# Reordering the opening of the product-key stage: batch norm first, its operands in the rows of the up-embedding buffer, that buffer loaded late in pieces, and small steps moved between engines

## The chip, the cores and the metric

The kernel runs on one core of one Trainium2 chip. The metric is the device time of one execution in microseconds (us); the times below are medians over runs of the same program. A trace of one profiled execution goes with it.

## What is computed

Two gated layers run over x (8 sequences of 512 tokens, 256 features): in each one a cross-attention and a feed-forward part, each added to x through a tanh gate. The change touches only the last part, a product-key memory of 4096 experts. Cut to that:

```python
def _L1_ffn_ref(x, w_q, bn_gamma, bn_beta, keys, down_embed, up_embed):
    q = jnp.einsum('bnd,de->bne', x, w_q)                       # 2048 columns
    mean = jnp.mean(q, axis=(0, 1)); var = jnp.var(q, axis=(0, 1))
    q = (q - mean) * jax.lax.rsqrt(var + BN_EPS) * bn_gamma + bn_beta
    q = q.reshape(b, n, 2, H, KD).transpose(2, 0, 1, 3, 4)
    sim = jnp.einsum('pbnhd,hkpd->pbnhk', q, keys)               # 2 x 8 heads x 64 keys
    sx, ix = jax.lax.top_k(sim[0], TOPK)
    sy, iy = jax.lax.top_k(sim[1], TOPK)
    all_scores = (sx[..., :, None] + sy[..., None, :]).reshape(b, n, H, TOPK * TOPK)
    scores, pk = jax.lax.top_k(all_scores, TOPK)
    ...
    h = gelu_new(jnp.einsum('bnd,bnhkd->bnhk', x, wd))
    h = jax.nn.softmax(scores, axis=-1) * h
    return jnp.einsum('bnhk,bnhkd->bnd', h, wu)
x = x + jnp.tanh(g_ffn[1]) * _L1_ffn_ref(_layernorm(x, axis=-1), ...)
```

## The kernel before

**The attention phase** (lines 129 to 1003) does everything up to the last feed-forward part, sequence by sequence. It leaves in DRAM the layer-normed tokens with features in the rows (`xT_d`), the residual (`x_d`), and for the first seven sequences the products of all tokens with all 4096 down-embeddings (`h_d`). In SBUF it leaves `gram`, the sum over all tokens of x times x, with the sums of x as a last column.

**The expert matrix is dense.** Experts are numbered 64 i + j. For a block of 256 tokens `gs[n]` holds the activation of all 4096 experts (rows: 64 experts j in each half of the 128 partitions, the halves for different tokens; columns: the 64 rows i times 128 tokens). The activations are multiplied with a dense weight made from the chosen experts, and contracted with `up_sb`, which holds the whole up-embedding (64 rows j, 64 i, 256 features; 4.19 MB) twice: once in partitions 0 to 63 and once in 64 to 127.

**`fold_phase`** opens the stage. It folds w_q, batch norm and keys into one matrix `mk` (256 x 1024) and one row `crow` (1024 constants), so that the scores of a tile of 128 tokens are one product. Its steps, each a group of instructions on TensorE with something behind it:
- `activations(i4)`, 16 of them: one 256 KB load of down-embeddings (`dwl`, two buffers), 32 matmul instructions (line 123) and four GELUs on ScalarE (line 1057). They make the `gs` of the last sequence, whose tokens arrive last (`xl`).
- four rounds over the columns of w_q (`wq`): the products `y` of gram and wq (line 1074), `z` = y times wq on VectorE (1078), and the column sums `sq` (1084).
- the batch norm chain: nine small steps on VectorE and one on GpSimd (1090 to 1104), which end in `ks` and `kh`.
- `pw` (1114), the folded product, copied to `mk` (1119); `pc` (1124), the constants, copied to `crow` (1128).

Two activations stand in each round, four between the batch norm chain and `pw`, and four at the end. The two loads of `up_sb` (line 1133) are issued on GpSimd's queue ahead of `fold_phase`.

**The tile loop.** There are 32 tiles p of 128 tokens, 16 blocks n of two tiles. For a tile: `similar` (scores on TensorE, lines 1162 and 1163, copied by ScalarE), `top` (MAX8 and FIND_INDEX8 over 64 keys, 16 times, 1175 and 1176), `choose` (sums of candidates `al`, then MAX8 and FIND_INDEX8 8 times, the shift `w` in 1195 and its exp), `places` (index arithmetic, softmax, `mlw`, and a transpose on TensorE, 1206 to 1239), `one_hot` four times (1250, 1252 on VectorE, 1253 on GpSimd), `weights_of` four times (`cf` on TensorE, 1263), `weigh` four times (1272). `finish` contracts a block with `up_sb` (`acc`, 1281) and `store` writes it. `fetch` and `apply` load and activate `h_d` of the block after next. The loop at line 1326 writes all of this out in an order that is two tiles ahead: at tile p it does `top`, `choose` and `places` of tile p + 2 and `similar` of tile p + 3. Ahead of the loop stand `similar`, `top`, `choose` and `places` of tiles 0 and 1, and `similar` of tile 2.

TensorE keeps the order in which the program is written (`ORDERED`, a manual schedule); the orders on the other engines and on the DMA queues come from a planner. Every engine carries out its own queue in order.

Of the kernel before, what the change touches and what calls it, by code (L numbers as in the profile page):

```python
# [10 lines left out]
F32 = mybir.dt.float32  # L11
# [25 lines left out]
def kernel(  # L37
# [978 lines left out]
    crow = p2.tile([1, 1024], F32, name="crow")  # L1016
# [15 lines left out]
    def fold_phase(ctx: ExitStack):  # L1032

        wp = ctx.enter_context(tc.tile_pool(name="wp", bufs=2))
        st = ctx.enter_context(tc.tile_pool(name="st", bufs=1))
        ps_h = ctx.enter_context(tc.tile_pool(name="ps_hl", bufs=2, space=PSUM))
        ps_y = ctx.enter_context(tc.tile_pool(name="ps_yf", bufs=2, space=PSUM))
        ps_s = ctx.enter_context(tc.tile_pool(name="ps_st", bufs=1, space=PSUM))

        xl = st.tile([P, NK, S], F32, name="xl")  # L1040
        nc.sync.dma_start(xl, xT_d[:, :, last * S : (last + 1) * S])
        bn_sb = st.tile([P, 32], F32, name="bn_sb")
        nc.scalar.dma_start(bn_sb, bn)
        kT = st.tile([P, 16, 64], F32, name="kT")
        nc.scalar.dma_start(kT, keysT)

        def activations(i4):

            dw = wp.tile([P, NK, 4, 64], F32, name="dwl")
            nc.sync.dma_start(dw, down[:, :, 4 * i4 : 4 * i4 + 4, :])  # L1050
            for i2 in range(2):
                ps = ps_h.tile([P, 2, 2 * P], F32, name="ps_hl")
                for ii in range(2):
                    expert_products(ps[:, ii, :], dw[:, :, 2 * i2 + ii, :], xl)
                for n in range(2):
                    i0 = 4 * i4 + 2 * i2
                    nc.scalar.activation(
                        gs[n][:, i0 : i0 + 2, :], ps[:, :, n * P : (n + 1) * P],
                        AF.Gelu_apprx_tanh,
                    )  # L1060


        sq = ps_s.tile([P, 16, 2], F32, name="sq")
        for n4 in range(4):
            wq = wp.tile([P, NK, 512], F32, name="wq")
            nc.scalar.dma_start(
                wq, pwq[:, 512 * n4 : 512 * (n4 + 1)].rearrange("(k p) n -> p k n", p=P)
            )
            z = wp.tile([P, NK, 512], F32, name="z")
            activations(2 * n4)  # L1070
            for k in range(NK):
                y = ps_y.tile([P, 512], F32, name="y", tag="y")
                for k2 in range(NK):
                    nc.tensor.matmul(
                        y, gram[:, k2, k * P : (k + 1) * P], wq[:, k2, :],
                        start=(k2 == 0), stop=(k2 == NK - 1),
                    )
                nc.vector.tensor_tensor(z[:, k, :], y, wq[:, k, :], ALU.mult)
            activations(2 * n4 + 1)
            for i in range(4):  # L1080
                n = 4 * n4 + i
                for j, (src, by) in enumerate(((z, None), (wq, gram))):
                    for k in range(NK):
                        nc.tensor.matmul(
                            sq[:, n, j : j + 1], src[:, k, i * P : (i + 1) * P],
                            ones[:, 0:1] if by is None else by[:, k, D : D + 1],
                            start=(k == 0), stop=(k == NK - 1),
                        )
        mv = st.tile([P, 16, 2], F32, name="mv")
        nc.vector.tensor_scalar(mv, sq, 1.0 / (NT * P), None, ALU.mult)  # L1090

        sc = st.tile([P, 16], F32, name="bn_sc")
        sh = st.tile([P, 16], F32, name="bn_sh")
        nc.vector.tensor_tensor(sc, mv[:, :, 1], mv[:, :, 1], ALU.mult)
        nc.vector.tensor_tensor(sc, mv[:, :, 0], sc, ALU.subtract)
        nc.vector.tensor_scalar(sc, sc, 0.0, EPS_LN, ALU.max, ALU.add)
        nc.gpsimd.tensor_tensor(sc, sc, mhalf.to_broadcast([P, 16]), ALU.pow)
        nc.vector.tensor_tensor(sc, sc, bn_sb[:, 0:16], ALU.mult)
        nc.vector.tensor_tensor(sh, sc, mv[:, :, 1], ALU.mult)
        nc.vector.tensor_tensor(sh, bn_sb[:, 16:32], sh, ALU.subtract)  # L1100
        ks = st.tile([P, 16, 64], F32, name="ks")
        nc.vector.tensor_tensor(ks, kT, sc.unsqueeze(2).to_broadcast([P, 16, 64]), ALU.mult)
        kh = st.tile([P, 16, 64], F32, name="kh")
        nc.vector.tensor_tensor(kh, kT, sh.unsqueeze(2).to_broadcast([P, 16, 64]), ALU.mult)
        for i4 in range(8, 12):
            activations(i4)
        for h in range(2):
            pw = [ps_y.tile([P, 8, 64], F32, name="pw", tag="y") for _ in range(NK)]
            for q4 in range(2):
                wT = wp.tile([P, 4, D], F32, name="wT")  # L1110
# [18 lines left out]
        for i4 in range(12, 16):  # L1129
            activations(i4)  # L1130
# [269 lines left out]
```

## Time and profile before

| What | Value |
|---|---|
| Median of 3 runs | 4431.82 us (4430.32 to 4437.95) |
| The profiled execution | 4438.74 us |
| Its span, first to last instruction | 4436.9 us |
| Busy: TensorE, VectorE, ScalarE, GpSimd | 85%, 56%, 36%, 14% of the span |
| Attention phase, to the last product of `gram` | 0 to about 3311 us |
| `fold_phase` on TensorE (first `ps_hl` to last) | 3314.6 to 3455.9 us |
| Tiles 0 and 1 ahead of the loop | 3458.6 to 3510.6 us |
| Tile loop, first `cf` to last `acc` | 3510.6 to 4430.6 us |

The page gives each engine's busy share over the span and in 40 slices of 111 us; the stage of this change is the last ten slices. Engines wait for one another by semaphores, so the question in each stretch is which wait ends last. The chain of waits follows that back from the last instruction; the timeline of one engine shows the waits in square brackets with what released them. The profiled execution lies 1.8 us above its span, and 6.9 us above the median.

### The profile page before, as it was taken

To read this page: it belongs to the slowest core of one execution; us is meant where nothing else is said; L and a number is where in the kernel's file an instruction comes from. 1 tells how busy PE (TensorE), PEld (TensorE's weight loads), DVE (VectorE), ACT (ScalarE), POOL (GpSimd) and SP (SyncE) were. 2 spreads that over 40 slices of the span, in tenths; PEclk is the share of its full clock that TensorE was granted. 3 is DMA by queue.
4 is the path that set the end of the run, shared out by engine and by line. 5 is a ranking of instruction groups with operands and counts; after the bars stand their busy time and mean duration, and the time that the engine had idled before them with its cause. 6 is when DMAs were issued, how large, how long until landed. Compare 5 with 4: busy or idle time off the path is not lost.

```text
span 4436.9 us, 74250 instructions
## 1 busy us (share of the span) xinstructions
PE 3779.7 (85%) x30697; PEld 1922.5 (43%) x30697; DVE 2473.8 (56%) x5662; ACT 1580.1 (36%) x2029; POOL 616.8 (14%) x613
## 2 busy tenths in 40 slices
PE   5678788889888998998898898789987589999998
PEld 2223332434334344434334434234445266666667
DVE  3455544454554454455445534553200699999995
ACT  2124343334443443453354343443431123333221
POOL 3210101020011012002001200000000122222222
PEclk7678998899999999999999999998997799999999
DMA  3201122123113313311321321103353022222221
GB/s 97 50 20 39 32 65 53 39 69 103 54 54 105 89 46 99 101 48 54 107 77 51 103 87 46 26 23 81 100 158 95 15 78 84 90 92 92 84 90 42
DMA packets 192254, 314.79 MB, mean 71 GB/s; under 512 B 20190, under 2 KB 145662, under 8 KB 184510
## 3 DMA queue, kind: packets, MB, share of 16 engines
q1 hardware_dynamic: 173468, 239.98, 18.0%
q0 software_dynamic: 15776, 65.02, 5.3%
q10 hardware_dynamic: 2672, 5.04, 0.4%
q8 instruction: 242, 3.96, 0.4%
q14 instruction: 96, 0.79, 0.1%
HBM read 220.93 MB, written 88.24 MB: 70 GB/s over the span
## 4 chain that ended last, share of the span: by engine, by line
PE 37%; DVE 17%; DMA 3%; ACT 1%; issue 1%; POOL 1%; SPq 0%; DVEq 0%; POOLq 0%; ACTq 0%
PE sc L331 10%; PE acc L1281 7%; PE ps_hd L123 6%; DVE nm L348 4%; PE av L391 3%; DVE m L1250 2%; DVE gs L1272 2%; DVE m L1252 2%; PE ps_y L707 1%; PE ps_hl L123 1%; DVE i L1176 1%; PE ps_h L690 1%; PE ps_sim L1162 1%; PE ps_q L293 1%; PE cf L1263 1%
## 5 line engine op out<-in xcount | busy, mean ns | idle before, releaser
L348 DVE TENSOR_REDUCE nm<-sc 128x2 f32<-128x1024 f32 x768 | 939.1, 1224 | 1047.0 <-PE sc L331 1043.2
L331 PE MATMUL sc<-ka,qa 32*128 32x512 f32 x3072 | 960.7, 684 | 297.4 <-DVE nm L348 284.4
L376 ACT ACTIVATE pr<-sc 128x1024 f32<-128x1024 f32 x768 | 785.9, 1024 | 1156.9 <-PE sc L331 1155.1
L331 PE MATMUL sc<-qa,ka 32*128 32x512 f32 x3072 | 917.8, 671 | 21.0 <-ACT pr L376 15.9
L331 PEld LDWEIGHTS sc<-ka,qa 32*128 32x128 f32 x3072 | 261.2, 194 | 722.7 <-DVE nm L348 535.8
L1281 PE MATMUL acc<-up_sb,gs 64*128 64x256 f32 x4096 | 489.9, 394 | 37.6 <-DVE gs L1272 37.6
L123 PE MATMUL ps_hd<-xT,dw 128*64 128x256 f32 x3584 | 439.0, 390 | 17.0 <-DMA dw<-in_down 6.5
L1281 PEld LDWEIGHTS acc<-up_sb,gs 64*128 64x128 f32 x4096 | 405.0, 195 | 93.3 <-DVE gs L1272 39.8
L391 PE MATMUL av<-pr,v 128*32 128x512 f32 x3072 | 436.6, 642 | 7.1 <-ACT pr L376 7.1
L1253 POOL TENSOR_TENSOR m<-m,chT 128x1024 f32<-128x1024 f32 x128 | 256.8, 2006 | 724.1 <-DVE m L1252 513.7
L123 PEld LDWEIGHTS ps_hd<-xT,dw 128*64 128x64 f32 x3584 | 247.1, 139 | 248.8 <-issue 117.9
L331 PEld LDWEIGHTS sc<-qa,ka 32*128 32x128 f32 x3072 | 246.8, 190 | 69.9 <-ACT pr L376 34.6
L823 ACT COPY hb<-ps_hd 128x512 f32<-128x512 f32 x224 | 130.8, 586 | 314.9 <-PE ps_hd L123 289.4
L542 ACT ACTIVATE pd<-mb,aT 128x512 f32<-128x512 f32 (+3 forms) x256 | 129.6, 553 | 211.2 <-PE cav L549 108.7
L391 PEld LDWEIGHTS av<-pr,v 128*32 128x32 f32 x3072 | 62.0, 110 | 320.2 <-issue 298.7
L534 POOL TENSOR_SCALAR_AFFINE_SELECT mb<-mb 128x256 f32<-128x256 f32 x128 | 52.2, 408 | 1010.9 <-DMA mb<-nM_d 572.8
L1263 PE MATMUL cf<-m,m 64*64 64x64 f32 x8192 | 156.1, 228 | 34.5 <-DVE gs L1272 29.0
L1263 PEld LDWEIGHTS cf<-m,m 64*64 64x64 f32 x8192 | 138.9, 141 | 101.4 <-issue 84.8
L1250 DVE TENSOR_TENSOR m<-chT,iota 128x1024 f32<-128x1024 f32 x128 | 169.8, 1326 | 2.0 <-ACT chT L1239 2.0
L569 DVE SCALAR_TENSOR_TENSOR pd<-csc,pd 128x512 f32<-128x512 f32 (+3 forms) x256 | 115.9, 486 | 94.3 <-PE csc L564 77.5
L1196 ACT ACT_TABLE_LOAD x28 | 35.9, 1283 | 366.5 <-DVE w L1195 354.3
L564 PE MATMUL csc<-qT,cT 32*128 32x256 f32 (+3 forms) x512 | 150.8, 567 | 10.8 <-DVE pd L569 7.2
(218 smaller groups left out, 4330.9 us busy)
## 6 DMA issues: line engine op xcount, KB each, us to landing
h_d<-hb SPq DMA_DIRECT2D x224, 256.0 KB
gs<-h_d SPq DMA_DIRECT2D x56, 1024.0 KB
dw<-in_down SPq DMA_DIRECT2D x112, 256.0 KB
w1e<-in_w POOLq DMA_DIRECT2D x16, 1024.0 KB, 5.4
w2e<-in_w POOLq DMA_DIRECT2D x16, 1024.0 KB, 6.3
mb<-nM_d SPq DMA_DIRECT2D x32, 512.0 KB
qk_d<-pk SPq DMA_DIRECT2D x64, 256.0 KB
ws<-in_w SPq DMA_DIRECT2D x56, 256.0 KB
```

The costliest lines, as they stand in the source:

```text
L123: nc.tensor.matmul(ps[64 * q : 64 * q + 64, :], dw[:, k, :], runs[:, :, q, :], start=(k == 0), stop=(k == NK - 1),)
L331: nc.tensor.matmul(sc[:, i, :], lhs[r : r + 32, g, c * P : (c + 1) * P], rhs[r : r + 32, g, :], start=True, stop=True,)
L348: nc.vector.tensor_reduce(self.nm[:, c, 2 * half : 2 * half + 2, g], sc, AX.X, ALU.max, negate=True)
L376: nc.scalar.activation(self.pr[jj], sc, AF.Exp)
L391: nc.tensor.matmul(self.av[32 * j : 32 * j + 32, :], self.va[:, c, h * (self.hd + 1) : h * (self.hd + 1) + 32], pr[j // 2][:, j % 2, :], s ...
L542: nc.scalar.activation(pds[c][:, i, s0:], mb[:, i, s0:], AF.Exp, bias=aT[:, c, h : h + 1])
L564: nc.tensor.matmul(sc[i][:, s0:], cT[r : r + 32, g, s0 : s0 + P], qT[r : r + 32, g, s0:], start=True, stop=True,)
L823: nc.scalar.copy(hb.rearrange("p n i t -> p i n t"), ps.rearrange("p i (n t) -> p i n t", n=2),)
L1250: nc.vector.tensor_tensor(m1, spread(0), grid, ALU.is_equal)
L1253: nc.gpsimd.tensor_tensor(m2, m2, spread(2), ALU.mult)
L1263: nc.tensor.matmul(cf[64 * q : 64 * q + 64, h, s, :], m2[rows, q, s, :], m1[rows, q, s, :], start=True, stop=True,)
L1281: nc.tensor.matmul(accs[n][q], gs[n % 2][rows, i, :], up_sb[rows, i, :], start=(i == 0), stop=(i == 63),)
```

## The change

`fold_phase` moves behind the functions of the tile loop, since it now calls them, and its order is new. Its operands (`xl`, `wq` four times, `z` twice, four `wT`, `kT`, `ks`, `kh`) no longer have buffers of their own but lie in `up_sb`, 4 KB per partition each, which `room(i, ...)` hands out as four of the 64 rows i. So `up_sb` can be loaded only once they are used up: in 16 loads of 512 KB (8 rows i, one half of the partitions), eight after activations 6 to 10 and eight after activations 11 to 15. In this phase the order on SP's queue is as written too.

The rounds have one activation each in place of two. The four activations between the batch norm chain and what follows it are gone; `pc` comes directly after the chain. `crow` becomes three rows of bf16, whose sum is the row (each the rounded rest of the one before), and the third matmul of `similar` takes three rows of bf16 in place of one of f32. Then come two activations, `pw`, and `similar`, `top` and `choose` of tiles 0 and 1; then five activations and `places` of tile 0 with the first eight loads, and the same for tile 1; then `similar` of tile 2.

In the functions of the tile loop four steps change engines: the shift `w` and the softmax product in `mlw` go from VectorE to GpSimd, the casts `kf` and `iv` from VectorE to ScalarE. `choose` makes its sums of candidates on VectorE in both kernels.

```diff
-    crow = p2.tile([1, 1024], F32, name="crow")
+    crow = p2.tile([3, 1024], BF16, name="crow")
+    ones3 = p2.tile([3, P], BF16, name="ones3")
...
-        nc.tensor.matmul(ps, ones[0:1, :], crow[:, cols], start=False, stop=True)
+        nc.tensor.matmul(ps, ones3, crow[:, cols], start=False, stop=True)
...
-        nc.vector.tensor_tensor(w, sc, sc[:, :, 0:1].to_broadcast([P, 8, 8]), ALU.subtract)
+        nc.gpsimd.tensor_tensor(w, sc, sc[:, :, 0:1].to_broadcast([P, 8, 8]), ALU.subtract)
...
-        nc.vector.tensor_copy(kf, ku)
+        nc.scalar.copy(kf, ku)
...
-        nc.vector.tensor_copy(iv, i8)
+        nc.scalar.copy(iv, i8)
...
-        nc.vector.tensor_tensor(
+        nc.gpsimd.tensor_tensor(
             mlw[:, 2, 0, :].rearrange("p (h k) -> p h k", k=8), w,
...
-    for q in range(2):
-        nc.gpsimd.dma_start(up_sb[64 * q : 64 * q + 64], up)
...
+        def room(i, shape):
+            axes = dict(zip("ab", shape))
+            return up_sb[:, 4 * i : 4 * i + 4, :].rearrange(
+                "p x y -> p (x y)"
+            ).rearrange("p (a b) -> p a b", **axes)
+        xl = room(15, (NK, S))
+        nc.sync.dma_start(xl, xT_d[:, :, last * S : (last + 1) * S])
+        wqs = [room(n4, (NK, 512)) for n4 in range(4)]
+        for n4, wq in enumerate(wqs):
+            nc.scalar.dma_start(
...
+            )
+        kT = room(14, (16, 64))
+        wTs = [room(6 + i, (4, D)) for i in range(4)]
+        for i, wT in enumerate(wTs):
+            nc.scalar.dma_start(wT, pwqT[:, 4 * i : 4 * i + 4, :])
...
+        for n4 in range(4):
+            wq = wqs[n4]
+            z = room(4 + n4 % 2, (NK, 512))
+            activations(n4)
...
+        ks = room(10, (16, 64))
+        kh = room(11, (16, 64))
+        for h in range(2):
+            pc = ps_y.tile([P, 512], F32, name="pc", tag="y")
+            nc.tensor.matmul(
+                pc[0:3], ones[:, 0:3], kh[:, 8 * h : 8 * h + 8, :].rearrange("p n i -> p (n i)"),
+                start=True, stop=True,
+            )
+            t0, t1 = (st.tile([3, 512], BF16, name=f"t{i}") for i in range(2))
+            rest = st.tile([3, 512], F32, name="rest")
+            nc.vector.tensor_copy(t0, pc[0:3])
+            nc.vector.tensor_tensor(rest, pc[0:3], t0, ALU.subtract)
+            nc.vector.tensor_copy(t1, rest)
+            nc.vector.tensor_tensor(rest, rest, t1, ALU.subtract)
+            nc.vector.tensor_scalar(rest, rest, ident[0:3, 2:3], None, ALU.mult)
+            for i, t in enumerate((t0, t1)):
+                nc.vector.scalar_tensor_tensor(
+                    rest if i == 0 else crow[:, 512 * h : 512 * h + 512],
+                    t, ident[0:3, i : i + 1], rest, ALU.mult, ALU.add,
+                )
+        activations(4)
+        activations(5)
...
+        for p in range(2):
+            for h in range(2):
+                similar(p, h)
+            for n0 in (0, 8):
+                top(p, n0)
+            choose(p)
+        for p in range(2):
+            for i4 in range(5 * p + 6, 5 * p + 11):
+                activations(i4)
+            places(p)
+            for i in range(32 * p, 32 * p + 32, 8):
+                for q in range(2):
+                    nc.sync.dma_start(
+                        up_sb[64 * q : 64 * q + 64, i : i + 8, :], up[:, i : i + 8, :]
+                    )
+        for h in range(2):
+            similar(2, h)
...
+        phase.enter_context(tc.manual_schedule(engines={mybir.EngineType.SP}))
+        fold_phase(phase)
...
-    for p in range(2):
-        for h in range(2):
-            similar(p, h)
-        for n0 in (0, 8):
-            top(p, n0)
-        choose(p)
-        places(p)
-    for h in range(2):
-        similar(2, h)
     one_hot(0, 0)
```

## The prediction

> **What bounds the kernel now.** I read the page first: its ten last slices are this stage, and in slice 31 TensorE falls to 4 tenths, VectorE to 0, while the DMA engines reach their highest rate. The chain of waits then gives the cause, in pieces of start, length and what ended.
>
> ```profile
> 3314.59 5.38 PE ps_hl L123 x32
> 3319.98 39.10 DMA dwl<-in_down
> 3359.22 5.70 PE ps_hl L123 x32
> ```
>
> An activation of 32 matmul instructions takes 5.4 us at a cold clock; the next but one waits 39 us for 256 KB of `dwl`. The view of the tile `up_sb` says what the DMA engines did meanwhile (two loads issued at 3312, 25.7 and 45.5 us to landing), the table of stretches how fast.
>
> ```profile
> L1133 POOL DMA_DIRECT2D up_sb<-in_up x2: 548/586/624, 3312.1 to 3312.7; - x2
> ...
> DMA to landing us min/median/max: 25.7/35.6/45.5
> ```
>
> ```profile
> 3340.00:3350.00 10.00, 0.00 (x0) 0.00 (x0) 0.00 (x0) 0.00 (x0) 0.00 (x0) 0.50 1.01 212
> ```
>
> No engine works from 3340 to 3350; 16 DMA engines are all busy and move only 212 GB/s. One half of `up_sb`, 4.19 MB, takes 45.5 + 0.6 - 25.7 = **20.4 us**.
>
> The second loss is in the timeline of TensorE: from 3458 to 3510 it is busy 27.5 of 52 us and waits for the VectorE chain of tiles 0 and 1 (`top`, `choose`, `places`), which runs beside nothing.
>
> ```profile
> 3477.76 0.90 PE L1236 MATMUL tr<-ident,mlw 128*128 128x128 f32 x3 [11.53 <-ACT mlw L1233]
> ...
> 3502.17 0.90 PE L1236 MATMUL tr<-ident,mlw 128*128 128x128 f32 x3 [12.38 <-ACT mlw L1233]
> ```
>
> Then the loop. In a stretch of two tiles VectorE is full and TensorE nearly:
>
> ```profile
> 3737.00:3794.00 57.00, 51.84 (x798) 38.31 (x798) 56.72 (x197) 17.43 (x24) 15.21 (x8) 0.94 0.26 88
> ```
>
> The columns are TensorE, its weight loads, VectorE (56.72 of 57), ScalarE, GpSimd. So the loop, 852 us from 3510 to 4362 for 30 tiles' worth of `choose` and `places`, is bound by **VectorE** first, 28.4 us a tile.
>
> **What the Trainium skill says of it.** "SBUF — State Buffer", section "Door 1: The DMA port swizzle": a transfer into 64 partitions reaches 8 of 16 ports, some 218 GB/s; the trace agrees (212). The same page, "Can I just issue two DMAs to hit both halves?": one transfer to each half gains only 6% over one alone, they serialize. The trace has the halves one after the other (4.19 MB in 20.4 us), not interleaved. The same page, "Who interferes with whom": casts in a 2-port mode on VectorE and a running GpSimd instruction block each other. That agrees: `iv` takes 0.19 us at its median and 1.93 where it starts inside a GpSimd product (3746.89, with line 1253 at work from 3746.51). "DMA: Bandwidth & Descriptors", section "Queues, rings and completion order": on each DMA engine a queue's descriptors are taken in ring order. Here it means that a load behind others on SP's queue comes last. The page also has the engines change between queues packet by packet; the 39 us of one `dwl` show that this shares nothing fairly against rows of 64 KB.
>
> **The change, part by part.** First the stretch from the first activation to the first `cf`: 3314.6 to 3510.6, **196 us** before.
>
> *Taken away:* the 39 us (27 idle, plus what stood ready behind). *Hidden:* 52 us of tiles 0 and 1; their VectorE work, some 21 us up to both `choose` (`top` 5.3, `choose` 3.4, twice, and the first scores), now runs beside five activations of 3.6 us. *Uncovered or added:* I lay TensorE's new order out with the durations of before.
>
> - Start: +4. The loads of `wq`, `wT` and `kT` are 4.7 MB, of which before 2 MB (two `wq`, two `wT`) came early, at 3267, and cost TensorE a wait of 5.67 us for `dw`. More may come there now, or later against `xl`: 0 to 8.
> - Four rounds of one activation (3.6), `y` (3.7), `sq` (3.7) and now an open wait for `z` (0.69 us and two handoffs: 1.0), which the second activation used to cover: 12.0, and the first cold +1.7; +1.3 for each of the others for a clock of 0.66 to 0.98 as in 3375 to 3400. Together 13.7 + 3 x 13.3 = 53.6.
> - Batch norm chain, 3409.8 to 3416.6, formerly under four activations: 6.8 bare.
> - `pc` 3.5 (half clock, as before). The splitting into three rows is 7 VectorE steps twice, nearest row the copy of `crow` at 0.68 us: at most 9.5 us, beside activations 4 and 5 (5.4 + 3.6 = 9.0) and `pw` (8.5), since only `similar` needs it. Nothing.
> - Four `similar`: two f32 products 1.91 (measured), the bf16 one 0.25: 8.7.
> - Activations 6 to 10: 18.0.
> - **First new wait.** SP issues the eight pieces after `dwl` 10, that is when activation 8 has freed a buffer. They are 4.19 MB into halves: 20.4 us, and `dwl` 11 is behind them on the same queue. It lands some 23 us after activation 8; activations 9 and 10 cover 7.2. Wait: 16. VectorE's chain for `places` 0 ends about when activation 10 does, so it adds nothing. What waits behind `dwl` 11: all of TensorE's order, the GELUs, `places` 1.
> - A transpose 0.5, activations 11 to 15: 5.7 cold + 14.4 = 20.6 in all.
> - **Second new wait.** Six pieces go out after activation 13, two after 15 (`xl` lies in their rows), and `xTt` of tile 2 is behind them: some 15.5 us after activation 15.
> - `similar` of tile 2, half cold: 6.
>
> Sum: 4 + 53.6 + 6.8 + 3.5 + 9 + 8.5 + 8.7 + 18 + 16 + 20.6 + 15.5 + 6 = 170, against 196: **-26**. Bounds: if the pieces flow at 350 GB/s (near the 363 seen at 3275 to 3280 into all partitions), both waits shrink by some 9: -45. If the buffer is held as a whole, so that pieces wait for every reader of it, each wait grows by some 8: -10. The three `one_hot` of VectorE that ran ahead before can run ahead here too, so the loop begins in the same state.
>
> *The loop, VectorE.* From the groups of lines between 3678 and 4360, 24 of each:
>
> ```profile
> L1212 DVE CAST iv<-i 128x128 bf16<-128x128 uint16 x24 | 23.7, 988 | 0.0
> L1210 DVE CAST kf<-ku 128x128 bf16<-128x128 uint32 x24 | 5.5, 227 | 0.8
> L1229 DVE TENSOR_TENSOR mlw<-w,sm 128x64 f32<-128x64 f32 x24 | 5.4, 225 | 0.8
> L1195 DVE TENSOR_TENSOR w<-psc 128x64 f32<-128x64 f32 x24 | 4.9, 205 | 0.0
> ```
>
> Removed a tile: 0.99 + 0.23 + 0.23 + 0.21 = 1.65 us. Behind `iv` comes MAX8 on one input, so most of its 0.8 us of blocking should go for good. Given back: `hot` waits for `kf`. On ScalarE that is about 0.3 us (the copy in line 1233 of 192 columns has 0.34) and two handoffs of 0.1, against 0.23 before: +0.3. The two products on GpSimd, about 0.3 us each, block the two-input products on VectorE when they meet: +0.3. The `exp` comes some 0.6 later, but its reader `sm` had 1.9 us in hand (3753.2 to 3755.1): nothing. `mlw` is 0.2 later to the transpose, for which TensorE has no wait in the loop. Net 1.05 x 30 = **-30**. Bounds: 1.65 x 30 plus half of VectorE's idle 12 us = -55; all eaten by waits, 0, or worse (below).
>
> *The loop, TensorE.* The bf16 product takes one pass: the skill's "TensorE: Matmul & The Clock Gate", section "Wait — 56ns, not 53.3ns?", has 216 ns for 512 bf16 columns, against 1.05 us in the chain: 0.8 x 2 a tile. The trace shows no bf16 product, so 0.24 to 0.96. TensorE falls from 50.4 to 47.3 us of 57; VectorE is the bound, so it is worth little by itself, but keeps TensorE from taking over.
>
> The last `finish` and `store` don't change. Sum against the profiled execution: 4438.7 - 26 - 30 = 4382.7. It stood 6.9 above the median, so I forecast 4431.8 - 56 = **4376**.
>
> **Rivals.**
> - *The waits are shorter than I think:* -45 and up to -52, 4335. For it: pieces alternate between halves. Against it: the page's 6%. 12%.
> - *The handoffs eat the loop's gain:* VectorE stands in its own order when ScalarE or GpSimd is late. -26 and 0: 4406. For it: an order planned with other durations. 17%.
> - *Slower:* `kf` falls in ScalarE's queue behind the burst of table load, `exp`, table load and two GELUs (1.28 + 0.26 + 1.28 + 2.0 = 4.8 us, from 3780.77). `hot` then waits some 4.5 a tile instead of 1.65 saved: +2.9 x 30 - 26 = +60, 4492. It decides from a wait of 1.65 + 26/30 = 2.5 us a tile. Against it: `ku` ends before the `exp` can begin, so the cast is ready first. 7%.
> - *The load is moved, not hidden:* whole-buffer waits and a colder clock leave the opening as it was, and the loop's gain is eaten: 4432. 4%.
>
> My forecast has 60%. Faster by over 0.2% (9 us, about what a measurement here can tell from no change): 0.6 + 0.12 + 0.17 = 0.89; same 0.04, slower 0.07. The range: 4335 to 4418, from the fast end of both bounds to the opening at -14 with an empty loop; the slower case is left out.
>
> **What would show it.** Right: no wait of 27 us for `dwl` 3; two waits of 13 to 17 us, for `dwl` 11 and for `xTt` of tile 2; a first `cf` near 3485; line 1163 at about 0.25 us, once; VectorE still at 98% in the loop, 27.4 us a tile. Wrong: VectorE idle before `hot` by more than 1 us a tile, a loop over 852 us, or a first `cf` before 3468 or after 3500.

## The result and the profile after

| | before | after |
|---|---|---|
| Median of 4 runs each | 4434.89 us (4430.32 to 4440.0) | 4380.07 us (4373.9 to 4385.84) |
| Ratio, with its 95% interval | 1 | 0.9876 (0.9855 to 0.9897) |
| The profiled execution, and its span | 4438.74, 4436.9 | 4385.84, 4384.1 |
| To the last `ot` product of attention | 3266.8 | 3262.1 |
| From there to the last product of `gram` (`ps_g`) | 44.3 | 38.3 |
| To the first activation of `fold_phase` | 3.5 | 9.7 |
| **The opening**: to the first `cf` | 196.0 | 174.7 |
| **The loop**: to the end of the span | 926.3 | 899.3 |

The changed kernel is 55 us faster by the medians. The profiled executions differ by 52.8 us: 21.3 in the opening, 27.0 in the loop, and 4.7 in attention, which the change doesn't touch (over all the profiled runs below the first activation starts between 3302.5 and 3322.3 us, so 4.7 is no gain). The two rows before the opening cancel out: -6.0 and +6.2.

In the kernel before, TensorE stood 27.0 us for one `dwl`, as its table of waits from 3310 to 3515 says (total us, times, longest):

```profile
PE ps_hl L123 <- DMA dwl<-in_down: 27.6, 2, 27.0
```

The chain of waits of the changed kernel no longer has a 39 us load. It has two of about half that, each behind pieces of `up_sb`:

```profile
3418.76 5.58 DMA up_sb<-in_up
3424.40 17.40 DMA dwl<-in_down
...
3462.90 14.95 DMA xTt<-xT_d
```

TensorE's timeline shows how long it stood for each of them (in brackets, with the releaser), and the small waits in between:

```profile
3321.01 0.38 PE L1198 MATMUL sq<-ones,up_sb 128*128 128x1 f32 x2 [0.67 <-DVE up_sb L1193]
...
3374.43 3.27 PE L1222 MATMUL pc<-up_sb,ones 128*3 128x512 f32 x4 [6.90 <-DVE up_sb L1218]
...
3414.61 10.54 PE L123 MATMUL ps_hl<-up_sb,dwl 128*64 128x256 f32 x80 [2.92 <-ACT gs L1175]
3441.93 12.42 PE L123 MATMUL ps_hl<-up_sb,dwl 128*64 128x256 f32 x96 [16.30 <-DMA dwl<-in_down]
3477.89 3.78 PE L1056 MATMUL ps_sim<-mk,xTt 128*128 128x512 f32 x4 [15.70 <-DMA xTt<-xT_d]
```

From above: the open wait for `z` in a round, the batch norm chain, a wait for the GELUs, and the two waits of 16 us for loads behind the pieces of `up_sb`. The table of stretches (TensorE, its weight loads, VectorE, ScalarE, GpSimd, clock, DMA share, GB/s) shows what holds these two, and then two tiles of the loop:

```profile
3426.00:3442.00 16.00, 0.07 (x2) 0.10 (x4) 10.31 (x6) 0.36 (x2) 7.46 (x3) 0.58 0.96 209
3462.00:3478.00 16.00, 0.30 (x3) 0.11 (x1) 0.00 (x0) 0.92 (x4) 0.00 (x0) 0.63 0.94 199
3738.00:3795.00 57.00, 50.65 (x804) 38.02 (x802) 54.31 (x199) 18.62 (x28) 18.46 (x13) 0.91 0.26 89
```

In both waits the DMA engines are full at about 200 GB/s. In the loop VectorE has fallen from 56.72 to 54.31 us of 57: it is no longer full. The table of waits, from 3660 to 4260 (total us, times, longest), says for what it and TensorE now stand:

```profile
PE tr L1130 <- ACT mlw L1127: 51.7, 11, 4.7
...
DVE s L1069 <- ACT sim L1058: 21.0, 13, 1.9
...
DVE hot L1110 <- ACT kf L1104: 5.5, 22, 0.5
```

The last line was forecast. The first was not: every second tile TensorE waits up to 4.7 us for `mlw` before its transposes, and the scores (`sim`) behind them come late to `top` on VectorE. Over the whole loop, first before and then after:

```profile
PE tr L1236 <- ACT mlw L1233: 19.7, 2, 9.9
...
DVE s L1175 <- ACT sim L1164: 12.5, 9, 2.6
...
PE tr L1130 <- ACT mlw L1127: 89.8, 16, 12.5
...
DVE s L1069 <- ACT sim L1058: 28.7, 18, 1.9
```

The timeline of GpSimd has the cause:

```profile
3753.31 1.90 POOL L1294 TENSOR_TENSOR m<-m,chT 128x1024 f32<-128x1024 f32 x1 [7.50 <-DVE sm L1122]
3755.17 1.27 POOL L1123 TENSOR_TENSOR mlw<-w,sm 128x64 f32<-128x64 f32 x1
```

The softmax product, now on GpSimd, is queued behind a product of `one_hot`, and takes 1.27 us where it takes 0.29 when VectorE leaves it alone.

### The profile page after: what moved, and what is told of

Same layout as the page of the kernel before. It is cut to its first block, busy times and chain, and to the rows that moved or that the text cites. A ratio compares the mean times of both kernels' runs of the same rounds, so it can differ in the third digit from the quotient of the medians.

```text
span 4384.1 us, 74170 instructions
## 1 busy us (share of the span) xinstructions
PE 3707.2 (85%) x30633; PEld 1891.7 (43%) x30633; DVE 2431.7 (55%) x5547; ACT 1599.8 (36%) x2097; POOL 647.7 (15%) x675
## 4 chain that ended last, share of the span: by engine, by line
PE 35%; DVE 17%; DMA 2%; ACT 2%; POOL 2%; issue 1%; SPq 0%; DVEq 0%; POOLq 0%; ACTq 0%
PE sc L331 10%; PE ps_hd L123 6%; DVE nm L348 4%; PE acc L1322 4%; PE av L391 3%; DVE m L1293 2%; DVE gs L1313 2%; PE ps_sim L1056 2%; DVE m L1291 2%; DVE i L1070 1%; PE ps_y L707 1%; PE ps_h L690 1%; PE ps_q L293 1%; PE ps_hl L123 1%; PE ps_p L282 1%
## 5 line engine op out<-in xcount | busy, mean ns | idle before, releaser
L331 PE MATMUL sc<-qa,ka 32*128 32x512 f32 x3072 | 913.7, 668 | 22.1 <-ACT pr L376 16.7
L1322 PE MATMUL acc<-up_sb,gs 64*128 64x256 f32 x4096 | 467.3, 381 | 1.5 <-DVE gs L1313 1.5
L1322 PEld LDWEIGHTS acc<-up_sb,gs 64*128 64x128 f32 x4096 | 389.3, 187 | 49.2 <-DVE gs L1313 1.7
L1056 PE MATMUL ps_sim<-mk,xTt 128*128 128x512 f32 x256 | 151.7, 723 | 15.7 <-DMA xTt<-xT_d 15.7
L1293 DVE TENSOR_TENSOR m<-chT,iota 128x1024 f32<-128x1024 f32 x128 | 161.5, 1262 | 0.0
L1291 DVE TENSOR_TENSOR m<-chT,iota 128x1024 f32<-128x1024 f32 x128 | 157.0, 1227 | 6.9 <-ACT chT L1133 6.9
```

Of the source, the lines that this page charges most:

```text
L331: nc.tensor.matmul(sc[:, i, :], lhs[r : r + 32, g, c * P : (c + 1) * P], rhs[r : r + 32, g, :], start=True, stop=True,)
L1056: nc.tensor.matmul(ps, xt[:, k, :], mk[:, k, cols], start=(k == 0), stop=False)
L1291: nc.vector.tensor_tensor(m1, spread(0), grid, ALU.is_equal)
L1293: nc.vector.tensor_tensor(m2, spread(1), grid, ALU.is_equal)
L1322: nc.tensor.matmul(accs[n][q], gs[n % 2][rows, i, :], up_sb[rows, i, :], start=(i == 0), stop=(i == 63),)
```

## The experiments

All against the kernel before on the same chip. A difference of two ratios counts only where it is clear of their intervals, some 0.001 to 0.003 to each side. The last column is the loop of the profiled run (first `cf` to the end of the span), split into what VectorE was busy and idle. That split is the tool for everything below: the loop is as long as VectorE's busy time plus its idle time, so a change must show in one of them.

| Kernel | Median us | Ratio (95%) | Opening | Loop = busy + idle |
|---|---|---|---|---|
| before | 4429.42 to 4442.93, by chip | 1 | 196.0 | 926.3 = 864.7 + 61.6 |
| the change | 4380.07 | 0.9876 (0.9855 to 0.9897) | 174.7 | 899.3 = 815.6 + 83.7 |
| opening_alone | 4416.15 | 0.9947 (0.9928 to 0.9965) | 177.5 | 933.1 = 872.0 + 61.1 |
| casts_back | 4421.88 | 0.9966 (0.9948 to 0.9983) | 172.3 | 937.4 = 846.8 + 90.6 |
| pool_back | 4442.67 | 1.0014 (0.9999 to 1.0028) | 171.9 | 958.3 = 857.8 + 100.5 |
| row_f32 | 4435.32 | 0.9999 (0.9990 to 1.0008) | 177.6 | 943.3 = 827.3 + 116.0 |
| soft_back | 4386.27 | 0.9890 (0.9858 to 0.9923) | 174.5 | 899.3 = 831.2 + 68.1 |
| late_turn | 4385.41 | 0.9897 (0.9866 to 0.9929) | 171.5 | 909.0 = 838.5 + 70.5 |
| wide_pieces | 4364.89 | 0.9840 (0.9807 to 0.9872) | 155.0 | 898.6 = 816.3 + 82.3 |
| spread_pieces | 4345.78 | 0.9803 (0.9770 to 0.9836) | 138.7 | 900.4 = 816.3 + 84.1 |
| late_turn1 | 4452.08 | 1.0025 (1.0014 to 1.0037) | 174.0 | 964.4 = 852.1 + 112.3 |
| row_turn1 | 4459.44 | 1.0034 (1.0021 to 1.0047) | 179.6 | 965.0 = 851.8 + 113.2 |
| pool_turn1 | 4484.87 | 1.0095 (1.0072 to 1.0118) | 171.5 | 990.1 = 859.4 + 130.7 |
| all_together | 4419.87 | 0.9936 (0.9913 to 0.9959) | 138.2 | 965.8 = 853.2 + 112.7 |

### The opening

**One part alone.** `opening_alone` has the new opening; the four steps go back to their engines and the row to f32.

```diff
-        nc.gpsimd.tensor_tensor(w, sc, sc[:, :, 0:1].to_broadcast([P, 8, 8]), ALU.subtract)
+        nc.vector.tensor_tensor(w, sc, sc[:, :, 0:1].to_broadcast([P, 8, 8]), ALU.subtract)
...
-        nc.scalar.copy(kf, ku)
+        nc.vector.tensor_copy(kf, ku)
...
-        nc.scalar.copy(iv, i8)
+        nc.vector.tensor_copy(iv, i8)
...
-        nc.gpsimd.tensor_tensor(
+        nc.vector.tensor_tensor(
             mlw[:, 2, 0, :].rearrange("p (h k) -> p h k", k=8), w,
...
-        nc.tensor.matmul(ps, ones3, crow[:, cols], start=False, stop=True)
+        nc.tensor.matmul(ps, ones[0:1, :], crow[:, cols], start=False, stop=True)
```

> The changed kernel with the loop's steps as before: the four small steps back on VectorE, the row of constants one row of f32. Only the new opening is left. Theory (two separate gains): the opening and what stands ahead of it is worth 26 us and the loop 27, so about 4434 - 26 = 4408, with a VectorE period of 28.4 us a tile again. Rival (the loop only became faster because it starts with more work done ahead): near 4380.

Measured: ratio 0.9947, so 0.0053 x 4435 = 23.5 us from the opening alone (15 to 32 by its interval); the other 0.0071 x 4435 = 31 us belong to the edits in the loop, given this opening. So both halves of the forecast are real, and the rival, that the loop gained only from its better start, is out. The size of the first half is less sure: in the profiled runs the opening is 18.5 us shorter, its six products of scores having the f32 row again, and the loop 6.8 us longer, since the cast `iv` meets GpSimd more often (33.6 us against 26.6).

**The two new waits.** `wide_pieces` loads into all 128 partitions, for which the input holds the up-embedding twice:

```diff
-                for q in range(2):
-                    nc.sync.dma_start(
-                        up_sb[64 * q : 64 * q + 64, i : i + 8, :], up[:, i : i + 8, :]
-                    )
+                nc.sync.dma_start(up_sb[:, i : i + 8, :], up[:, i : i + 8, :])
```

> The changed kernel with the 16 loads of up_sb into 64 partitions replaced by 8 loads of 1 MB into all 128 (the input is laid out twice, one copy for each half), at the same places of SP's queue. Theory (the two new waits of the opening are as long as the pieces are slow, 205 GB/s into 64 partitions): at about 350 GB/s the 4.2 MB take 12 instead of 20 us, the wait for dwl 11 falls from 16.3 to 8 and that for xTt of tile 2 from 15.7 to 7.5, the time by 16, to about 4364. Rival (the rate comes from the alternation of rows, or the pieces wait for buffers rather than for the DMA engines): both waits stay within 2 us of what they are, and the time at 4380.

Its timeline of TensorE has the same two waits at less than half:

```profile
3433.36 12.08 PE L123 MATMUL ps_hl<-up_sb,dwl 128*64 128x256 f32 x96 [6.52 <-DMA dwl<-in_down]
...
3460.28 3.69 PE L1056 MATMUL ps_sim<-mk,xTt 128*128 128x512 f32 x4 [6.86 <-DMA xTt<-xT_d]
```

Between 3422 and 3434 its DMA engines moved 382 GB/s. So the length of the waits is the bytes of the pieces over their rate: 16.3 + 15.7 became 6.5 + 6.9, and the opening is 19.7 us shorter, where 16 were expected.

`spread_pieces` keeps the 64 partitions and moves the loads apart:

```diff
+            if n4 == 1:
+                piece(48, 56)
+            if n4 == 3:
+                piece(0, 8)
...
+        piece(8, 16)
+        piece(16, 24)
+        after = {7: (24, 32), 8: (32, 40), 9: (40, 48), 10: (56, 60)}
...
+                if i4 in after:
+                    piece(*after[i4])
...
+        piece(60, 64)
```

> The changed kernel with the same 16 loads of 64 partitions, but each pair issued as soon as its rows of up_sb are used up: one in the second round, one in the fourth, two after the second choose, then one after each of activations 7 to 9, the rest after activation 10 and after xTt of tile 2. Theory (the two waits come from eight pieces standing ahead of dwl 11 and of xTt on one queue): both waits of about 16 us go, of which some 3 to 6 us come back as shorter waits for single pieces, and the time falls by 24 to 32, to about 4350. Rival (what the pieces take of the DMA engines is taken from the activations' own loads wherever they stand): as many waits, only shorter each, and the time within 8 us of 4380.

The first wait is gone: activation 11 starts right behind the transposes, and the next wait, of 0.69 us, comes before activation 14. The second is gone too:

```profile
3426.47 10.58 PE L123 MATMUL ps_hl<-up_sb,dwl 128*64 128x256 f32 x96
3437.75 7.13 PE L123 MATMUL ps_hl<-up_sb,dwl 128*64 128x256 f32 x64 [0.69 <-DMA dwl<-in_down]
...
3445.19 1.88 PE L1056 MATMUL ps_sim<-mk,xTt 128*128 128x512 f32 x4
```

The opening is 36.0 us shorter than the change's, more than was expected, and the loop is as it was. 32.0 of them are the two waits; most of the rest comes from the products behind them, which are no longer slow (12.42 to 10.58 us, 3.78 to 1.88). The bytes are the same, and so are the 64 partitions that each piece goes into; what differs is when the pieces are issued. So the 32 us came from eight pieces at a time standing ahead of one small load, and how long such a wait is, their rate decides. The packets of the changed kernel show the order itself: `dwl` 11 was issued at 3424.40, yet none of its packets of 1 KB starts before 3438, when the pieces are nearly through. That another queue for the pieces would have helped was not run. In the kernel before they were on GpSimd's queue, and a `dwl` on SP's took 39.10 us beside them. This is the fastest version that was run: 4345.78 us.

### The loop: one edit undone at a time

`casts_back` puts `kf` and `iv` back on VectorE:

```diff
-        nc.scalar.copy(kf, ku)
+        nc.vector.tensor_copy(kf, ku)
...
-        nc.scalar.copy(iv, i8)
+        nc.vector.tensor_copy(iv, i8)
```

> The changed kernel with the two casts kf and iv back on VectorE. Theory: the loop is bound by VectorE, and iv costs it 0.99 us a tile (0.19 of work and 0.8 blocked by GpSimd), kf 0.23, less 0.25 that it now waits for kf: +0.97 x 30 = +29 us, 4409. Rival (blocking only moves elsewhere): iv counts its 0.19 alone, +5 us, 4385.

The loop is 38.1 us longer: 31.2 of busy time and 6.9 of idle time. That is near the theory and far from the rival, but not by the theory's sum. The cast is blocked at some meetings with GpSimd, though less than before. The group of lines from 3660 to 4260:

```profile
L1106 DVE CAST iv<-i 128x128 bf16<-128x128 uint16 x21 | 12.7, 604 | 0.0
```

Over the loop the two casts take 26.4 us, where the theory had 36.6. The rest came from elsewhere: the `m` steps (the two comparisons of `one_hot`, 1291 and 1293) took 316.7 us against 307.8, and VectorE waited 41.7 us for scores against 28.7.

`row_f32` puts the row back to one f32 matmul, at line 1055 of that kernel:

```diff
-        nc.tensor.matmul(ps, ones3, crow[:, cols], start=False, stop=True)
+        nc.tensor.matmul(ps, ones[0:1, :], crow[:, cols], start=False, stop=True)
```

> The changed kernel with the row of constants as one row of f32 again. TensorE gets some 0.7 us more in each of 64 products, 1.4 us a tile. Theory (VectorE bounds the loop): +0 to +10 us, 4380 to 4390. Rival (TensorE bounds at least half of the loop): +1.4 x 30 = +42, 4422.

The rival was right: the loop's whole gain is lost, and more. The edit only adds 0.73 us to a product on TensorE (1.05 in place of 0.32 from its start to the next), 58 times in the loop: 42 us, and the loop is 44.0 longer. In the table of waits of 3660 to 4260 one sees the path:

```profile
PE tr L1128 <- ACT mlw L1125: 47.0, 10, 4.7
DVE s L1067 <- ACT sim L1056: 42.7, 18, 3.1
```

VectorE waits 42.7 us for the scores, twice what it did. Over the loop its idle time is 32.3 us longer, all of it for scores (61.1 against 28.7), and its busy time 11.7 (the `m` steps). So in the changed kernel **TensorE's order, its work and its wait for `mlw`, sets the pace** together with VectorE. One thing is not separated here: the planner gave VectorE another order too, in which 16 of the 250 `m` steps take over 1.5 us, where the change has 3. So the 44 us are the row together with the order that came with it.

`pool_back` puts the shift `w` and the softmax product of `mlw` back on VectorE:

```diff
-        nc.gpsimd.tensor_tensor(w, sc, sc[:, :, 0:1].to_broadcast([P, 8, 8]), ALU.subtract)
+        nc.vector.tensor_tensor(w, sc, sc[:, :, 0:1].to_broadcast([P, 8, 8]), ALU.subtract)
...
-        nc.gpsimd.tensor_tensor(
+        nc.vector.tensor_tensor(
             mlw[:, 2, 0, :].rearrange("p (h k) -> p h k", k=8), w,
```

> The changed kernel with the shift w and the softmax product of mlw back on VectorE, the casts on ScalarE. Theory: VectorE gets 0.43 us a tile more (+13 us), but TensorE's wait of 4.7 us in every second tile for the transpose behind GpSimd's product goes, and with it most of VectorE's new idle time of 0.78 us a tile (-14 to -23): 4370 to 4380, the same or faster than the changed kernel. Rival (VectorE's work alone counts): +13, 4393.

Both expectations missed: the loop is 59.0 us longer, 42.2 of it busy time, where the rival had 13. The trace shows three things that neither had. The first is on ScalarE and VectorE (one timeline):

```profile
3727.58 1.28 ACT L1090 ACT_TABLE_LOAD   x1 [5.41 <-DVE w L1089]
...
3729.16 0.22 DVE L1121 TENSOR_REDUCE sm<-w 128x8 f32<-128x64 f32 x1 [1.45 <-ACT w L1090]
```

When `w` comes from VectorE, the table load for the exp waits for it, 1.28 us ahead of the exp. `sm`, the sum over that exp, waits 1.45 us a tile, 39.4 in the loop. When `w` comes from GpSimd the load goes out early. But `w` comes from VectorE in the kernel before and in `opening_alone` too, and there `sm` has no wait at all: from the fourth tile of the loop on nine steps stand on VectorE's queue between `w` and `sm`, where in `pool_back`, as in the changed kernel's order, only the two `ku` steps do. So this wait, too, belongs to the edit in this order and not to the edit alone. The second: the product `hot<-hot,iv` takes 774 ns at its mean from 3660 to 4260 and 417 in the changed kernel, 19.5 us in the loop. The third: the softmax product takes 773 ns at its mean in the loop, where it took 224 before, 16.5 us.

`soft_back` is half of that, the softmax product alone:

```diff
-        nc.gpsimd.tensor_tensor(
+        nc.vector.tensor_tensor(
             mlw[:, 2, 0, :].rearrange("p (h k) -> p h k", k=8), w,
```

> The changed kernel with only the softmax product of mlw back on VectorE; the shift w stays on GpSimd. Theory (what made the kernel with both back lose 59 us is the table load of exp, which waits for w on VectorE and holds sm back by 1.45 us a tile): here the table load still goes early, so the time is 4380 to 4395 and VectorE doesn't wait for w before sm. Rival (what cost is the product on VectorE itself, 0.81 us at its mean where GpSimd blocks it, and the hot products beside it): most of the 59 us is here too, 4415 to 4440.

The theory was right: +0.0014 in the ratio, less than the intervals, and a loop of the same 899.3 us. Busy time rises by 15.6 us and idle time falls by as much, since TensorE's wait for `mlw` goes down from 89.8 to 43.4 us in the loop. So, with the other edits in place, the move of this product to GpSimd gave nothing that can be told from none: what VectorE saved came back as its wait for scores (28.7 us against 15.5). VectorE's order is the changed kernel's here with this one step put in, so no other order is mixed in. The loss of `pool_back` came with the move of `w` and the order planned for it.

### Is TensorE's wait worth taking away?

`late_turn` lets the transposes wait where nobody needs them yet:

```diff
+        mlws[p] = mlw
+
+    def turn(p):
+
+        mlw = mlws.pop(p)
         tr = ps_t.tile([P, 4, P], F32, name="tr", tag="s")
...
             weigh(p, u, cf)
+            if u == 0 and 0 < p < NP - 1:
+                turn(p + 1)
```

> The changed kernel, but the three transposes of a tile (and the two copies of their result) stand one step later in TensorE's order: after the first cf and weigh of the next tile, not in the middle of places. Nothing is added or left out. Theory (in the changed kernel TensorE's order, its work and its waits, sets the pace of the loop): its wait of 4.7 us for mlw in every second tile, 51.7 us in the stretch 3660 to 4260 and some 70 in the whole loop, goes; another wait takes over part of it, so the time falls by 30 to 60, to about 4320 to 4350, and VectorE's busy share in that stretch rises from 95.5 to over 97%. Rival (VectorE sets the pace, TensorE's waits are slack): within 10 us of 4380, and TensorE waits just as long for something else.

The wait for `mlw` is gone (4.2 us in the loop for 89.8), and the time is the rival's: 4385 us. But not for the rival's reason. VectorE's idle time is 13.2 us shorter, as the theory has it in kind, though it had 30 to 60; its busy time is 22.9 longer, and 19.6 of that are `hot<-hot,iv`, a product of two inputs in `places`. The timelines of VectorE and GpSimd, one after the other:

```profile
3710.85 1.22 DVE L1300 TENSOR_TENSOR m<-chT,iota 128x1024 f32<-128x1024 f32 x1
3711.99 0.68 DVE L1120 TENSOR_REDUCE mlw<-hot 128x64 f32<-128x512 bf16 x1
3712.58 1.84 DVE L1116 TENSOR_TENSOR hot<-hot,iv 128x512 bf16<-128x512 bf16 x1
...
3712.24 1.90 POOL L1301 TENSOR_TENSOR m<-m,chT 128x1024 f32<-128x1024 f32 x1 [5.16 <-DVE m L1300]
```

The planner, given other code, placed this product just behind the `m` pair that starts GpSimd's product, and it stands until that ends: 1.84 us in place of 0.42. In VectorE's order 13 of 64 of these products stand so in `late_turn` and in `pool_back`, and none in before, the change, `casts_back`, `row_f32` and `soft_back`. 13 x 1.42 = 18.5 us, nearly all that these products lost in both. The Trainium skill, "SBUF — State Buffer", section "Who interferes with whom", has two-input instructions on VectorE contend with a GpSimd instruction that reads SBUF, and the order of issue decide which of them stands; the trace agrees.

Four more kernels used an order without these. `late_turn1` has the transposes two steps later (the lines are against `late_turn`):

```diff
-            if u == 0 and 0 < p < NP - 1:
+            if u == 1 and 0 < p < NP - 1:
                 turn(p + 1)
```

> The changed kernel with the transposes of a tile two steps later (after the second cf and weigh of the next tile; late_turn had them after the first). Nothing is left out. In VectorE's order of late_turn 13 of 64 products hot<-hot,iv stood right behind the m pair whose GpSimd product then runs, and took 1.84 in place of 0.42 us; in the changed kernel and in this one none stands there. Theory (late_turn did take away a wait that sets the pace, 13 us of VectorE's idle time, and lost it again to 20 us of those blocked products): hot<-hot,iv is back at 0.42 us, VectorE's wait for sim is under 15 us in the stretch 3660 to 4260, and the time is 10 to 20 us below the changed kernel's, 4360 to 4370. Rival (TensorE's wait is slack): within 8 us of 4380 though the products are not blocked.

Neither: 4452 us. The blocked products are gone (22.6 us in the loop, as in the change), and so is the wait for scores. But two steps are one too many:

```profile
DVE m L1298 <- ACT chT L1139: 43.9, 20, 3.7
```

VectorE now stands for the transposed result (`chT`) in 29 of 30 tiles, 63.0 us in the loop, and its `m` steps meet GpSimd's products more often (344.0 us against 307.8). So this run doesn't tell what the loop would be with neither loss.

`row_turn1` and `pool_turn1` put the f32 row, or the two products on VectorE, into `late_turn1`, by the diffs of `row_f32` and `pool_back`.

> As late_turn1 and with the f32 row of before in place of the three bf16 rows. Theory (the f32 row cost 44 us because TensorE, with its products and its wait for mlw, set the pace; with that wait gone TensorE has slack): it costs less than half of that, 0 to 20 us above late_turn1, some 4365 to 4385. Rival (the row's 0.73 us are on the path wherever the transposes stand): 40 to 48 us above late_turn1, some 4405 to 4415.

As the theory has it: the row costs 0.6 us in the loop and 0.0009 in the ratio, less than the intervals, where it cost 44 us before. Here VectorE stands for `chT` and TensorE has slack: one of its waits ahead of `cf` falls from 85.8 to 38.7 us as the row takes its time out of it. The same edit is worth 44 us or nothing, by who sets the pace.

> As late_turn1 and with both two-input products, the shift w and the softmax product of mlw, back on VectorE. In its order too no product hot<-hot,iv stands behind the m pair. Theory (of the 59 us that this cost before, 20 were those blocked products, which came with the planner's order and not with the edit, the rest the product's 0.2 to 0.8 us and the wait of sm for the table load behind w): 25 to 40 us above late_turn1, 4390 to 4405. Rival (all of it belongs to the edit): 50 to 65 us above late_turn1, 4415 to 4430.

0.0070 x 4435 = 31 us above `late_turn1`, within the theory's 25 to 40; the loop of the profiled run is 25.7 us longer. But the split is not the theory's. Of the 59 us of `pool_back`, two parts are missing here: the blocked `hot<-hot,iv` (19.5) and the longer softmax product, which takes 220 ns at its mean in place of 773. `sm` again waits 39.4 us for the exp, and 13.9 of that come off VectorE's wait for `chT`. So the order made more of the loss than the 20 us, and what the edit costs by itself isn't shown.

`all_together` joins the two kinds of pieces, a later load of `wT`, and `late_turn1` (the lines are against `spread_pieces`):

```diff
         def piece(i0, i1):
-            for q in range(2):
-                nc.sync.dma_start(
-                    up_sb[64 * q : 64 * q + 64, i0:i1, :], up[:, i0:i1, :]
-                )
+            nc.sync.dma_start(up_sb[:, i0:i1, :], up[:, i0:i1, :])
...
+            if n4 == 2:
+                for i, wT in enumerate(wTs):
+                    nc.sync.dma_start(wT, pwqT[:, 4 * i : 4 * i + 4, :])
```

> What the runs point to, in one kernel: the changed kernel with the transposes as in late_turn1, the loads of up_sb into all 128 partitions (8 of them, one of these in two parts) and each issued as soon as its rows are free, and the four loads of wT issued in the third round of SP's queue and not at the start. Theory (gains of different stretches add): the opening gives 36 to 42, the later wT some 4, the loop 10 to 20, together 50 to 66 below the changed kernel, 4315 to 4330. Rival (what the opening gains the loop loses, since VectorE's work of the first tiles no longer stands beside waits): 4340 to 4350, no better than spread_pieces.

Neither theory nor rival: it is slower than `spread_pieces`, and slower than the change. The opening keeps what `spread_pieces` had, 138.2 us, and no more: with the loads apart, their rate no longer matters. The later `wT` gave nothing, for TensorE waits 9.25 us before the first activation as against 9.37. The loop brings with it the 66 us of the late transposes, so the theory's 10 to 20 us for the loop had the wrong sign.

## Why the prediction was right, and where not

The forecast was 4376 us, within 4335 to 4418, from a median before of 4431.82; the median is 4380.07, and with a fourth run the kernel before has 4434.89. So 55 us were gained where 56 were forecast. The opening was right by its mechanism. In the loop the sum was right, but single terms were not, and their errors nearly cancel. By its own steps:

- **The load of `up_sb` leaves the path: right.** The `dwl` of 39.10 us, for which TensorE stood 27.0, is gone.
- **Two new waits of 16 and 15.5: right**, 16.30 and 15.70, at 209 and 199 GB/s where the forecast took 20.4 us for 4.19 MB (205). `wide_pieces` shows the rate at work, `spread_pieces` the place of the pieces ahead of the small loads. The rival of shorter waits (pieces that alternate between the halves gain rate) is refuted by the 209.
- **Start +4: about 0.** The first activation waits 9.4 us for its `dwl` beside the other loads, but those that came early before, and held TensorE for 5.67, now come later: -6.0 and +6.2.
- **The rounds 53.6: 57.4.** The open wait is 0.67 (forecast 1.0 with its handoffs); the products at the cold clock were sized short, in the first round (15.9 us for 13.7) and in the last (15.1 for 13.3). The batch norm chain, 6.8, took 6.9.
- **Activations 6 to 10 at 18.0: 24.2.** This step missed a wait. `choose` of tiles 0 and 1 puts an exp, which needs another table, between the GELUs, and the forecast looked at the burst of table loads only for `kf` in the loop. ScalarE's timeline:

```profile
3409.98 1.28 ACT L1090 ACT_TABLE_LOAD   x1
3412.61 0.26 ACT L1090 ACTIVATE w<-w 128x64 f32<-128x64 f32 x1 [1.35 <-POOL w L1089]
3412.88 1.28 ACT L1175 ACT_TABLE_LOAD   x1
3414.18 0.94 ACT L1175 ACTIVATE gs<-ps_hl 128x256 f32<-128x256 f32 x3
```

The table is switched at 3409.98, then the exp waits for GpSimd's `w`, and the GELUs for which TensorE waits stand behind both: waits of 1.28, 0.25 and 2.92, and the products behind the last are slow. With `w` and the casts back on VectorE, in `opening_alone`, 0.61 and 2.32 of such waits remain. Activations 4 and 5, `pw` and 11 to 15 with the transposes came 3.5 us shorter together (34.6 against 38.1).
- **The opening -26: -21.3**, first `cf` at 3484.8, forecast near 3485. That it hit so closely is luck: attention ended 4.7 us earlier in this execution.
- **VectorE sheds 1.65 us a tile, 49.5 in all: 49.1 of busy time, but not as reckoned.** The four groups were 46.2 us long in the loop of before. Records on VectorE overlap by some 0.08 us (in the changed kernel `ku` starts at 3717.81, takes 0.19, and the next starts at 3717.92), so removing four saves about 0.3 a tile less than their means add up to. The `m` steps made up for it: 319.9 to 307.8 us, for 17 of the 250 took over 1.5 us before, each begun inside a GpSimd product, and 3 after. This wasn't forecast.
- **Given back 0.3 for `kf`: 0.22** (6.7 us in the loop). **0.3 for blocking by the two new products: not seen on VectorE.** It is GpSimd's product that was blocked, 1.27 for 0.29.
- **"`mlw` is 0.2 later to the transpose, for which TensorE has no wait in the loop": wrong.** This wait rose from 19.7 to 89.8 us. It is the 4.7 above, and what came of it on VectorE is 16.2 us more waiting for scores (12.5 to 28.7). With the 6.7 for `kf` this is about the 22 us by which idle time grew. So 49.1 - 22.1 = 27.0, against a forecast of 30 (its own 1.05 x 30 is 31.5). The forecast gave back 9 for blocking, which did not come, and nothing for the wait for scores, which took 16.2; that the sum is near is in part luck.
- **The bf16 row "worth little by itself": wrong in its size; "keeps TensorE from taking over": right.** Taking it out costs 44 us, with the order that comes with it. The step read VectorE's 98% as the bound and TensorE's 50.4 of 57 us as room (the stretch that it shows has 51.84); once VectorE was relieved by 1.65 us a tile, the room was gone, since TensorE also stands for `mlw` and VectorE for the scores. The product itself takes 0.32 us from its start to the next, where the forecast took 0.25.
- **VectorE at 98% in the loop: 95% (54.31 of 57).** The forecast's own mark of "wrong" was idle time before `hot` of over 1 us a tile; the idle time came, 0.7 a tile, but most of it before `top`.

The slower rival, `kf` behind ScalarE's burst, did not come: 0.22 us a tile against its threshold of 2.5.

What the single edits of the loop are worth cannot be added: undone one at a time, they cost 38 (casts), 59 (the two products) and 44 us (row), yet undone together 34. Each undone alone leaves another engine or another order in charge. That the planner's order took some 20 us of `pool_back` and of `late_turn` is shown by the blocked products. Of the runs that undo edits, only `soft_back` leaves the rest of VectorE's order in place, so the price of the other edits alone stays open, and so does what the loop would be with `late_turn` and no blocked products.

## What to carry to other kernels

When a large load stands ahead of small ones that are needed soon, first place it between them as its room comes free: that gave 36 us of the opening here, while nearly twice the rate gave 20. In the loop of before VectorE was busy 93% and TensorE 89% of the time, and of 49.1 us taken from VectorE only 27.0 were gained. So where two engines are nearly full, lay out both engines' orders with their waits, and ask of each moved step what stands behind it on its new queue. Compare kernels by busy time plus idle time of one engine: this separates a new wait from steps that have become longer by contention, which a changed order can bring without any edit to them.

## What was not expected of the hardware

After a wait of some length TensorE is slower for a while, and this adds to the price of the wait. In one pair of tiles of the changed kernel's loop:

```profile
3747.07 1.98 PE L1056 MATMUL ps_sim<-mk,xTt 128*128 128x512 f32 x4
...
3756.88 0.90 PE L1130 MATMUL tr<-ident,mlw 128*128 128x128 f32 x3 [4.70 <-ACT mlw L1127]
3757.58 3.62 PE L1056 MATMUL ps_sim<-mk,xTt 128*128 128x512 f32 x4
```

The same four products take 1.98 us when TensorE comes from work, and 3.62 behind the wait of 4.70. Together with the transposes (0.90, and 0.55 elsewhere) the wait costs at least 2 us more than its length. The Trainium skill, "TensorE: Matmul & The Clock Gate", section "Part 1: The HAM clock gate (the "warmup" mystery)", has an idle TensorE fall to half its clock after some 3.4 us; this pair agrees. A wait isn't needed, though. Two activations of the opening, the first right behind the one-column products `sq`, the second behind `similar`:

```profile
3326.01 5.37 PE L123 MATMUL ps_hl<-up_sb,dwl 128*64 128x256 f32 x32
...
3400.87 3.67 PE L123 MATMUL ps_hl<-up_sb,dwl 128*64 128x256 f32 x32
```

TensorE had no wait before either.

The second is the table load's place: it goes out early when the exp waits for GpSimd (3409.98, and the exp at 3412.61), but waits for `w` itself when `w` comes from VectorE (`pool_back`, and the kernel before). Why is not shown. It costs only where the reader of the exp stands close behind: 1.45 us a tile in `pool_back`, nothing in the kernel before.
